# Four fused image layers on one core: the order and spacing of a wavelet layer's column products, and the start of the last pair's layers

## The chip, the cores and the metric

The kernel runs on one core of a Trainium2 chip. The core has five engines, each with its own instruction queue, worked off in order: TensorE (PE; its weight loads are listed apart as PEld), VectorE (DVE), ScalarE (ACT), GpSimd (POOL) and SyncE (SP), which here only issues DMAs. Engines wait for one another through semaphores. Data lies in SBUF (128 partitions) and in PSUM, where TensorE writes its sums; sixteen DMA engines move data between DRAM and SBUF.

The metric is the device time of one execution in microseconds. Comparisons use medians of several runs.

## What is computed

Four layers, each on a group-normalized input and added back to it. The input is 8 images of 64 channels, 128 x 128, in float32.

```python
# layer 0: adder convolution, 3x3
out[o] = relu(b[o] - abs(patches - w[o]).sum(-1))
# layer 1: spline activation for each channel
out = scale_base * silu(x) + scale_sp * einsum('bhwck,ck->bhwc', bspline_basis(x), coef) + bias
# layer 2: wavelet convolution
ll, ch, cv, cd = haar_dwt(x)                     # 4 subbands of 64 x 64
t = stack of the 4 subbands, transposed          # 256 channels
t = conv2d(t, dw_w, dw_b, groups=256, pad=1)     # depthwise 3x3
t = conv2d(t, pw_w, pw_b, pad=0)                 # 256 -> 256, 1x1
t = conv2d(t, cv_w, cv_b, pad=1)                 # 256 -> 256, 3x3
out = haar_idwt(gelu(t), transposed back)
# layer 3: nearest of 512 embeddings for each pixel
out = embed_weight[argmin(squared_dist(x_pixel, embed_weight))]

x = x + layer0(gn(x)); x = x + layer1(gn(x)); x = x + layer2(gn(x)); x = x + layer3(gn(x))
```

## The kernel before

Two images lie on the 128 partitions (2 x 64 channels): a pair. Four pairs are worked off.

**Layer 0 and its planner.** The adder layer takes by far the most time. ScalarE makes |x - w| for one channel and tap as a tile of 128 x 4096 (L821), VectorE makes maxima max(x, w) (L774) or a maximum fused with an addition (L844); TensorE sums the 64 channels of each tile with a selecting matrix into PSUM (L809). `layer0` holds a planner: clocks for PE, ACT and DVE, advanced by assumed costs (`COSTS` and constants), pick which engine gets the next tile and write the instruction order of the three engines out by hand. Some nine tiles (`buf`, `wide`, x) are in flight. A pass (16 output channels of a chunk of 32 rows) has 144 taps (`TAPS`).

**Layers beside it.** While layer 0 of pair n runs, layers 1 to 3 of pair n-1 run beside it in generators that are advanced in *steps*: `STEPS` gives the steps of layer 1, layer 2, the statistics of a raw pair and layer 3. The steps are spread evenly over the 16 passes of a pair (L755 to L757), so that one step comes about every two taps. Each generator notes its events under step numbers (`at(step, f, ...)`), and `spread_out` issues them in the order of the steps on all engines.

**Layer 2 beside.** `layer2_beside` works on 8 chunks of 16 image rows, `EACH` = 56 steps apart (b is a chunk's first step). For a chunk: `load` brings input rows (xin, one buffer), `columns` and `rows` make the subbands on VectorE, `depthwise` their 3 x 3 sums on VectorE. The 1 x 1 and 3 x 3 convolutions are one, by a fast scheme along the columns (an even and an odd output column from four products): `columns_of` makes the input v of product kind m (one buffer), `products` multiplies it on TensorE with weights u, which `load_u2` brings from DRAM for each of the 16 product events of a chunk (384 KB, one buffer, so a load waits until the product before it is done). A kind's four events gather in one PSUM tile `mm` (one buffer); the `take_` functions move it into g: `take_first` to `take_fourth` for kinds 0 to 3. Then come `gelu` on ScalarE, `inverse` (wavelet back) on TensorE, `add` to xa on VectorE, statistics, and `store`, a DMA to x_dram; xa (one buffer) is loaded by `load_x`. All these loads and stores are issued by SP, in the order that a scheduler gives them, and so are layer 0's stores of y (L673) and of channel sums (L621) and loads of st (L631).

**Last pair.** After layer 0 has ended, `layer1`, `layer2` and `layer3` work on the last pair alone, with all of its x in SBUF. `layer1` takes 16 units (half chunks); TensorE forms its sums in pa and pb (L953). `layer2` starts with `haar` of the first chunk and the first four rows of the second, put between the steps of the group norm; then `begin` (ACT) and `depthwise` (DVE) for each subband (KS = 1, 2, 3, 0), `products` for one half of the output bands (`oab`), and so on; its PSUM holds three tiles of two banks (`l2_ps`) and two of one bank (`l2_pi`). `take` moves a half into g, `two_inverses` and `two_adds` finish the chunk before. `layer3` prepares four rows first (`prepare`, `squares`, `take_squares`), then goes row by row: TensorE distances (L1227), ScalarE and VectorE the smallest (L1233, L1237, L1241), GpSimd fetches the embedding (L1242).

## Time and profile before

| what | us |
|---|---|
| three runs | 18358.89, 18349.82, 18328.94 (median 18349.82) |
| the profiled execution | 18391.41 |
| its span, first to last instruction | 18389.7 |
| first pair's layer 0 alone | about 0 to 3640 |
| layers 0 and beside it layers 1 to 3 of three pairs | about 3640 to 17274 |
| of that, layer 2 beside | about 4547 to 6480, 9150 to 11110, 13800 to 15740 |
| last pair alone: layer 1 | 17274 to 17535 |
| last pair alone: layer 2 | 17535 to 17977 |
| last pair alone: layer 3 | 17977 to 18390 |

The mean granted TensorE clock was 0.985 of full speed. A row of the groups by line gives line, engine, operation, the tiles written and read, shape and count; then busy time and the mean of one in ns; then the idle time of the engine just before these instructions and who ended it. "SPq" marks the issue of a DMA by SP, not its transfer. In a timeline a row has the start, the length, the instruction, and in brackets the idle time before it.

### The profile page before, as it was taken

What the parts mean: (1) busy time and instruction counts of PE and PEld (TensorE: products, weight loads), DVE (VectorE), ACT (ScalarE), POOL (GpSimd) and SP (SyncE); (2) the same over time, 40 slices, a digit from 0 to 9 for tenths busy, and PEclk for the clock granted to TensorE, in tenths of its full rate; (3) what the DMA queues carried; (4) which work ended last, traced back from release to release, by engine and by line L of the source; (5) the groups of instructions that cost most, each with busy time, mean ns of one, the idle gap of its engine ahead of it and who ended that gap; (6) DMA issues with size and microseconds to landing.
All of it is one profiled execution on the core that took longest, in us unless ns stands there. A gap on an engine that the chain in (4) does not pass through costs nothing.

```text
span 18389.7 us, 338059 instructions
## 1 busy us (share of the span) xinstructions
PE 17822.3 (97%) x150418; PEld 6142.1 (33%) x150418; DVE 17676.9 (96%) x13410; ACT 17162.3 (93%) x6556; POOL 3386.7 (18%) x1866
## 2 busy tenths in 40 slices
PE   8999999999999999999999999999999999999998
PEld 2222222222333323332233333233223333222364
DVE  8999999999999999999999999999999999999887
ACT  7999999999999999999999999999999999999924
POOL 1222222200000024430000002443000000344205
PEclk9999999999999999999999999999999999999997
DMA  7767777611111111011111111101111111110231
GB/s 146 132 124 137 132 130 137 130 40 40 43 48 49 44 39 26 23 31 38 41 41 48 53 43 39 29 23 29 42 39 44 45 53 43 28 28 21 66 107 42
DMA packets 454213, 1099.90 MB, mean 60 GB/s; under 512 B 72416, under 2 KB 234848, under 8 KB 395360
## 3 DMA queue, kind: packets, MB, share of 16 engines
q0 software_dynamic: 111792, 491.89, 15.2%
q1 hardware_dynamic: 340960, 586.39, 11.2%
q8 instruction: 1178, 19.30, 0.4%
q14 instruction: 283, 2.32, 0.0%
HBM read 526.58 MB, written 125.74 MB: 35 GB/s over the span
## 4 chain that ended last, share of the span: by engine, by line
PE 54%; DVE 26%; issue 11%; ACT 6%; DMA 2%; POOL 1%; SPq 0%; DVEq 0%; another core or an unknown queue 0%; ACTq 0%; POOLq 0%
PE ps L809 41%; DVE buf L774 13%; ACT buf L821 4%; PE mm L1511 4%; DVE buf L844 4%; PE pd L1666 2%; DVE r L1353 1%; DVE wide L774 1%; PE ps L1227 1%; PE m L1079 1%; DMA u<-u_dram 1%; DVE dw L1484 1%; DVE nd L1678 1%; DVE x L774 1%; PE pa L953 0%
## 5 line engine op out<-in xcount | busy, mean ns | idle before, releaser
L809 PE MATMUL ps<-buf,sel 128*32 128x512 f32 x112848 | 12574.1, 595 | 168.4 <-ACT buf L821 87.6
L821 ACT ACTIVATE buf<-wide,w 128x4096 f32<-128x4096 f32 x1901 | 6922.4, 3711 | 80.1 <-PE ps L809 79.3
L821 ACT ACTIVATE buf<-x,w 128x4096 f32<-128x4096 f32 x1823 | 6647.1, 3711 | 129.3 <-PE ps L809 123.6
L809 PEld LDWEIGHTS ps<-buf,sel 128*32 128x32 f32 x112848 | 3540.5, 110 | 8634.0 <-issue 7801.0
L774 DVE TENSOR_SCALAR buf<-x,w 128x4096 f32<-128x4096 f32 x1801 | 4166.2, 2357 | 75.2 <-PE ps L809 68.8
L774 DVE TENSOR_SCALAR buf<-wide,w 128x4096 f32<-128x4096 f32 x1731 | 4028.8, 2367 | 95.3 <-PE ps L809 89.7
L1681 POOL DMA_INDIRECT g<-in_L_conv_embed_weight,ix x768 | 1860.2, 2422 | 2390.0 <-issue 1170.8
L844 DVE SCALAR_TENSOR_TENSOR buf<-x,w,buf 128x4096 f32<-128x4096 f32 x440 | 1973.3, 4485 | 15.7
L658 POOL DMA_DIRECT2D y<-in_x x496 | 704.9, 2173 | 6961.4 <-ACT y L645 5343.3
L844 DVE SCALAR_TENSOR_TENSOR buf<-wide,w,buf 128x4096 f32<-128x4096 f32 x430 | 1928.4, 4485 | 15.3
L1511 PE MATMUL mm<-v,u 64*128 64x256 f32 x9216 | 1182.0, 401 | 142.1 <-DMA u<-u_dram 129.1
L1511 PEld LDWEIGHTS mm<-v,u 64*128 64x128 f32 x9216 | 893.4, 195 | 557.4 <-issue 239.3
L832 POOL DMA_DIRECT2D buf<-buf x203 | 508.0, 2503 | 2739.6 <-DVE buf L774 2363.2
L821 ACT ACTIVATE x<-wide,w 128x4096 f32<-128x4096 f32 x263 | 975.9, 3711 | 5.8 <-PE ps L809 5.8
L821 ACT ACTIVATE wide<-x,w 128x4096 f32<-128x4096 f32 x259 | 961.1, 3711 | 4.8 <-PE ps L809 4.8
L809 PE MATMUL ps<-wide,sel 128*32 128x512 f32 x7696 | 923.1, 594 | 11.4 <-ACT wide L821 4.6
L809 PE MATMUL ps<-x,sel 128*32 128x512 f32 x7776 | 927.2, 593 | 3.3 <-ACT x L821 1.9
L1484 DVE SCALAR_TENSOR_TENSOR dw<-sub,dws,dw 128x512 f32<-128x512 f32 (+2 forms) x768 | 573.4, 747 | 10.4
L1668 ACT ACTIVATE t<-emb,xsq 128x512 f32<-128x512 f32 x768 | 512.2, 718 | 42.3 <-DVE xsq L1659 23.8
L1678 DVE CUSTOM_DVE_ANT_0 nd<-pd,t 128x512 f32<-128x512 f32 x768 | 519.6, 677 | 32.5 <-ACT t L1668 17.0
L774 DVE TENSOR_SCALAR x<-wide,w 128x4096 f32<-128x4096 f32 x223 | 529.5, 2374 | 8.9 <-PE ps L809 8.8
L1680 DVE FIND_INDEX8 ix<-best,nd 128x8 uint32<-128x512 f32 x768 | 526.2, 685 | 0.0
(288 smaller groups left out, 10465.5 us busy)
## 6 DMA issues: line engine op xcount, KB each, us to landing
buf<-buf POOLq DMA_DIRECT2D x203, 2048.0 KB
u<-u_dram SPq DMA_DIRECT2D x512, 384.0 KB
z<-x_dram SPq DMA_DIRECT2D x192, 256.0 KB
x<-x_dram SPq DMA_DIRECT2D x96, 512.0 KB
raw<-in_x SPq DMA_DIRECT2D x32, 1024.0 KB
x_dram<-y SPq DMA_DIRECT2D x512, 64.0 KB
y<-in_x POOLq DMA_DIRECT2D x496, 64.0 KB
x_dram<-x SPq DMA_DIRECT2D x48, 512.0 KB
```

The source lines that it names most:

```text
L658: nc.gpsimd.dma_start(out=ys[p][at], in_=d, accum_op=ALU.add)
L774: nc.vector.tensor_scalar(ab, tap(p // OG, t), w[:, t : t + 1], None, ALU.max)
L809: nc.tensor.matmul(to, sel[:, M - 1 - m : 3 * M - 1 - m], rhs, start=(done % TAPS == 0), stop=((done + span) % TAPS == 0))
L821: nc.scalar.activation(ab, tap(p // OG, t), AF.Abs, bias=w[:, t : t + 1], scale=-1.0)
L832: nc.gpsimd.dma_start(out=into, in_=of, accum_op=ALU.add, max_dma_last_dim=8192)
L844: nc.vector.scalar_tensor_tensor(ab, tap(p // OG, t), w[:, t : t + 1], ab, ALU.max, ALU.add)
L1484: nc.vector.scalar_tensor_tensor(out, v, wt, out, ALU.mult, ALU.add)
L1511: nc.tensor.matmul(ps[:, i], u2[r, k % 2, di, :], vs[c, m][r, k, di : di + G, :], start=(k == 0 and di == 0), stop=(k == 3 and di == 2))
L1668: nc.scalar.activation(t, emb[:, 1], AF.Identity, bias=xsqs[j][:, n : n + 1])
L1678: nc.vector.tensor_tensor_reduce(nd, ps, t, 1.0, -FAR, ALU.subtract, ALU.max, mx[:, 0:1])
L1680: nc.vector.max_index(ix, mx, nd)
L1681: nc.gpsimd.indirect_dma_start(out=g[:, img, :], out_offset=None, in_=self.embed, in_offset=bass.IndirectOffsetOnAxis(ap=ix[:, 0:1], axis=0),)
```

## The change

Beside layer 0, a chunk's products are put three steps apart instead of two, a kind every 14 steps instead of 11, and the steps behind them (gelu, inverse, add, store) 12 later; layer 2 gets 514 steps. Kind 1, which goes into both columns, comes first: `take_first` makes both copies of it on ScalarE, `take_second` adds kind 0 to the even column.

In the last pair, the first wavelet rows are issued ahead of layer 1's last unit, in a pool of their own, and a small Silu activation ahead of layer 1; unit 0 of layer 1 has two ramps on VectorE instead of ScalarE. In layer 2 the first chunk is multiplied band by band for both halves, the second band by band for its first half; all PSUM tiles are of one kind (four of two banks). The last chunk's statistics are taken in two parts. Layer 3 prepares two rows first, then two, then four.

```diff
-STEPS = (208, 500, 24, 396)
+STEPS = (208, 514, 24, 396)
...
     "layer2_beside.products": {"PE": 2.95},
-    "layer2_beside.take_first": {"ACT": 1.0},
-    "layer2_beside.take_second": {"DVE": 1.18, "ACT": 1.0},
+    "layer2_beside.take_first": {"ACT": 2.0},
+    "layer2_beside.take_second": {"DVE": 1.18},
     "layer2_beside.take_third": {"DVE": 2.36},
     "layer2_beside.take_fourth": {"DVE": 1.18},
...
+                if n == 2 * NCH - 1:
+                    for part in first_rows:
+                        next(part)
...
-                        on_act = p < 1 + i
+                        on_act = p < (1 + i if n else 1 - i)
...
+    def haar(self, n, lo, hi, row, pool):
+        nc, S = self.nc, HW2
+        sub, inner = self.sub, slice(1, S + 1)
+        xv = self.x[n][:, lo:hi]
+        s, d = (pool.tile([P, R, S], F32, name=name, bufs=2)[:, 0 : hi - lo] for name in ("hs", "hd"))
+        nc.vector.tensor_tensor(s, xv[:, :, 0:W:2], xv[:, :, 1:W:2], ALU.add)
+        nc.vector.tensor_tensor(d, xv[:, :, 0:W:2], xv[:, :, 1:W:2], ALU.subtract)
+        out = [sub[:, k, row : row + (hi - lo) // 2, inner] for k in range(4)]
+        nc.vector.tensor_tensor(out[1], s[:, 0 : hi - lo : 2], s[:, 1 : hi - lo : 2], ALU.subtract)
+        nc.vector.tensor_tensor(out[2], d[:, 0 : hi - lo : 2], d[:, 1 : hi - lo : 2], ALU.add)
+        nc.vector.tensor_tensor(out[3], d[:, 0 : hi - lo : 2], d[:, 1 : hi - lo : 2], ALU.subtract)
+        yield
+        nc.vector.scalar_tensor_tensor(out[0], s[:, 0 : hi - lo : 2], self.m4, s[:, 1 : hi - lo : 2], ALU.add, ALU.add)
+        yield
+
+    def first_rows(self, pool):
+        S, G = HW2, R // 2
+        self.sub = pool.tile([P, 4, G + 3, S + 2], F32, name="sub")
+        self.m4 = pool.tile([P, 1], F32, name="m4")
+        self.nc.gpsimd.memset(self.sub[:, :, :, 0 : S + 2 : S + 1], 0.0)
+        self.nc.gpsimd.memset(self.sub[:, :, 0, 1 : S + 1], 0.0)
+        self.first_parts = [self.haar(0, 0, R, 1, pool), self.haar(1, 0, 4, 1 + G, pool)]
...
-            first = [haar(0, 0, R, 1), haar(1, 0, 4, 1 + G)]
-            fill = [part for part in first for _ in range(6)]
             mr = self.mr_tile()
             with tc.tile_pool(name="gn_ps", bufs=1, space=PSUM) as pg:
                 for _ in self.group_norm_steps(stats_in, mr, pg):
-                    for _ in range(2):
-                        if fill:
-                            next(fill.pop(0))
-            for part in fill:
-                next(part)
+                    pass
...
-            pp = ctx.enter_context(tc.tile_pool(name="l2_ps", bufs=3, space=PSUM))
-            pi = ctx.enter_context(tc.tile_pool(name="l2_pi", bufs=2, space=PSUM))
+            nc.vector.tensor_scalar(self.m4, mr[:, 0:1], -4.0, None, ALU.mult)
+
+            pp = ctx.enter_context(tc.tile_pool(name="l2_ps", bufs=4, space=PSUM))
...
-            def convolve(j, oab):
+            def convolve(j, oab, by_band=False):
                 pairs = open_pairs()
-                for n in range(2):
-                    for k in KS:
-                        products(j, oab, pairs, n, k)
+                order = [(n, k) for k in KS for n in range(2)] if by_band else [(n, k) for n in range(2) for k in KS]
+                for n, k in order:
+                    products(j, oab, pairs, n, k)
                 return pairs
...
+            def open_inverses(at):
+                both = pp.tile([P, 2, 2, G, S // 2], F32, name="m").rearrange("p a b r c -> p a (b r c)")
+                return {pos: both[:, n].rearrange("p (r c) -> p r c", c=S) for n, pos in enumerate(at)}
+
             def two_inverses(j, gs, at):
-                pys = {}
+                pys = open_inverses(at)
                 for pos in at:
-                    pys[pos] = pi.tile([P, G, S], F32, name="py")
                     for ab in range(2):
                         inverse(pys[pos], gs, pos, ab)
...
             begin(0, KS[:3])
-            pairs = open_pairs()
+            halves = [open_pairs() for _ in range(2)]
             for n, k in enumerate(KS):
                 if n == 3:
                     for part in first:
                         next(part, None)
                     begin(0, KS[3:])
                 depthwise(0, k)
-                for half in range(2):
-                    products(0, 0, pairs, half, k)
-            late = None
-            for j in range(NCH):
+                for oab, pairs in enumerate(halves):
+                    for half in range(2):
+                        products(0, oab, pairs, half, k)
+            transform(1)
+            begin(1, KS)
+            gs = []
+            for n, k in enumerate(KS):
+                depthwise(1, k)
+                if n in (1, 2):
+                    gs.append(take(halves[n - 1], n - 1))
+            late = (0, gs)
+            for j in range(1, NCH):
                 more = list(KS) if j + 1 < NCH else []
-                if j > 0:
-                    pairs = convolve(j, 0)
+                pairs = convolve(j, 0, j == 1)
                 if more:
                     transform(j + 1)
                     begin(j + 1, KS)
-                    for k in more[: 1 if j == 0 else 2]:
+                    for k in more[:2]:
                         depthwise(j + 1, k)
-                    del more[: 1 if j == 0 else 2]
-                if late:
-                    pys = two_inverses(*late, (0, 1))
+                pys = two_inverses(*late, (0, 1))
                 gs = [take(pairs, 0)]
-                if late:
-                    two_adds(j - 1, pys)
+                two_adds(j - 1, pys)
                 pairs = convolve(j, 1)
-                for k in more[:2]:
+                for k in more[2:]:
                     depthwise(j + 1, k)
-                del more[:2]
-                if late:
-                    pys = two_inverses(*late, (2, 3))
+                pys = two_inverses(*late, (2, 3))
                 gs.append(take(pairs, 1))
-                if late:
-                    two_adds(j - 1, pys)
-                for k in more:
-                    depthwise(j + 1, k)
-                if late:
-                    self.chunk_stats(stats, j - 1)
+                two_adds(j - 1, pys)
...
-            both = pp.tile([P, 2, 2, G, S // 2], F32, name="m").rearrange("p a b r c -> p a (b r c)")
-            pys = [pi.tile([P, G, S], F32, name="py") for _ in range(2)]
-            pys += [both[:, n].rearrange("p (r c) -> p r c", c=S) for n in range(2)]
+            pys = {**open_inverses((0, 1)), **open_inverses((2, 3))}
             for ab in range(2):
                 for pos in range(4):
                     inverse(pys[pos], gs, pos, ab)
+            by_parity = self.x[j].rearrange("p (r a) w -> p a r w", a=2)
             for pos in range(4):
                 add(j, pys[pos], pos)
-            self.chunk_stats(stats, j)
+                if pos % 2:
+                    for half in range(2):
+                        nc.vector.bn_stats(stats[:, 4 * j + pos - 1 + half, :], by_parity[:, pos // 2, half * G // 2 : (half + 1) * G // 2])
...
-            prepare(0, 0)
-            squares(0, 0, 4)
-            take_squares(0, 0, 4)
+            prepare(0, 0, 2)
+            squares(0, 0, 2)
+            take_squares(0, 0, 2)
+            prepare(0, 2, 2)
             prepare(0, 4)
             for n in range(NCH * R + LATE):
                 j, r = divmod(n, R)
-                if j == 0 and r in (1, 5, 9):
-                    squares(0, r + 3, r + 7)
-                    take_squares(0, r + 3, r + 7)
-                    if r < 9:
-                        prepare(0, r + 7)
+                if j == 0 and r in (1, 2, 5, 9):
+                    lo, hi = {1: (2, 4), 2: (4, 8)}.get(r, (r + 3, r + 7))
+                    squares(0, lo, hi)
+                    take_squares(0, lo, hi)
+                    if 1 < r < 9:
+                        prepare(0, hi)
...
             def take_first(c):
                 gs[c] = sp.tile([P, 2, 2, G, S], F32, name="g")
-                nc.scalar.copy(even_and_odd(c)[0], product_of(c, 0))
+                ps = product_of(c, 1)
+                for to in even_and_odd(c):
+                    nc.scalar.copy(to, ps)
 
             def take_second(c):
-                even, odd = even_and_odd(c)
-                ps = product_of(c, 1)
-                nc.vector.tensor_tensor(even, even, ps, ALU.add)
-                nc.scalar.copy(odd, ps)
+                even = even_and_odd(c)[0]
+                nc.vector.tensor_tensor(even, even, product_of(c, 0), ALU.add)
...
                     c = j - 1
-                    when = [(b + 11 * m + 3 + 2 * n, c, m, n // 2, n % 2) for m in range(4) for n in range(4)]
+                    kinds = ((1, take_first), (0, take_second), (2, take_third), (3, take_fourth))
+                    when = [(b + 14 * at_m + 3 + 3 * n, c, m, n // 2, n % 2) for at_m, (m, _) in enumerate(kinds) for n in range(4)]
                     for n, (step, *what) in enumerate(when):
                         at(when[n - 1][0] + 1 if n else b - 3, load_u2, *what)
                         at(step, products, *what)
-                    for m, take in enumerate((take_first, take_second, take_third, take_fourth)):
-                        at(b + 11 * m, columns_of, c, m)
-                        at(b + 11 * m + 11, take, c)
+                    for at_m, (m, take) in enumerate(kinds):
+                        at(b + 14 * at_m, columns_of, c, m)
+                        at(b + 14 * at_m + 15, take, c)
                     for oab in range(2):
-                        at(b + 46, gelu, c, oab)
+                        at(b + 58, gelu, c, oab)
                     for a in range(2):
-                        s = b + 48 + 9 * a
+                        s = b + 60 + 9 * a
                         at(s - (8 if a == 0 else 1), load_x, c, a, 0)
...
+            with tc.tile_pool(name="l2_first", bufs=1) as pool:
+                warm = self.small.tile([P, 1], F32, name="warm", tag="warm", bufs=1)
+                self.nc.scalar.activation(warm, self.bias1, AF.Silu)
+                later = self.stats_tile("later")
+                self.layer1(self.group_norm(stats.pop(last), by_tile=True), later, self.first_rows(pool))
+                self.early.close()
+                between = self.stats_tile("between")
+                self.layer2(later, between, pool)
             self.layer3(between, last)
```

Where lines are left out, the old inner function haar of layer2 and its memsets moved into the two new functions unchanged in what they compute, and calls pass the new pool.

## The prediction, made before the changed kernel was run

> **What bounds the kernel now.** I read the page first (engines, then the costliest groups), then the groups by line beyond it, then busy time by windows, then the instructions and waits of tile u, then the timeline of single waits.
>
> ```profile
> PE 17822.3 (97%) x150418; PEld 6142.1 (33%) x150418; DVE 17676.9 (96%) x13410; ACT 17162.3 (93%) x6556; POOL 3386.7 (18%) x1866
> ...
> L1511 PE MATMUL mm<-v,u 64*128 64x256 f32 x9216 | 1182.0, 401 | 142.1 <-DMA u<-u_dram 129.1 <-issue 5.8 <-ACT g L1537 4.1
> ```
>
> Three engines are nearly full, so only idle time that they share is worth anything. TensorE (PE) has 567 us of it, and one line, the products of layer 2, owns 142.1 us: TensorE stands waiting for the weights u to arrive from DRAM.
>
> ```profile
> 4547.00:6480.00 1933.00, 1872.38 (x16424) 731.92 (x16420) 1855.73 (x1149) 1835.95 (x543) 81.43 (x65) 0.98 0.17 46
> ...
> 6700.00:8200.00 1500.00, 1494.60 (x12749) 452.20 (x12753) 1481.26 (x1525) 1492.59 (x646) 689.51 (x305) 1.00 0.11 26
> ```
> ```profile
> 5213.00:5390.00 177.00, 177.00 (x1576) 69.60 (x1576) 174.92 (x108) 176.79 (x52) 0.00 (x0) 1.00 0.15 41
> ```
>
> Busy time by windows (length, then PE, PEld, DVE, ACT, POOL, clock, DMA). The first is layer 2 of the first pair beside the adder layer, the second layer 3 beside it: 97% of PE against 99.6%. The third lies inside layer 2 and has no wait for u: PE is full, ScalarE (ACT) and VectorE (DVE) almost. So the waits are the loss, and without them TensorE is the bound.
>
> ```profile
> 5186.45 0.33 SPq L1451 DMA_DIRECT2D xin<-x_dram  x1
> 5188.75 0.37 SPq L1574 DMA_DIRECT2D x_dram<-xa  x1
> 5191.10 0.37 SPq L1558 DMA_DIRECT2D xa<-x_dram  x1
> 5191.57 8.01 SPq L1500 DMA_DIRECT2D u<-u_dram  x2
> ```
> ```profile
> 5182.99 5.36 PE L809 MATMUL ps<-buf,sel 128*32 128x512 f32 x48
> 5194.92 4.29 PE L1511 MATMUL mm<-v,u 64*128 64x256 f32 x24 [6.56 <-DMA u<-u_dram]
> ```
>
> One wait, on SP's queue and on PE. The previous product had ended at 5183.0, so u's single buffer was free; but the load stood in SP's queue behind xin (waits for VectorE's rows), a store (waits for VectorE's additions at 5188.7) and xa (waits for that store to land, 2.3 us). It was issued at 5191.57 and landed 3.3 us later.
>
> ```profile
> L1511 PE MATMUL mm<-v,u x9216: 373/376/793, 4708.0 to 15641.2; 64*128 64x256 f32 x197
> ...
> PE mm L1511: 129.1, 42
> ```
> ```profile
> L1537 ACT COPY g<-mm 128x1024 f32<-128x1024 f32 x24 | 28.0, 1167 | 96.1 <-DVE g L1536 96.1
> ```
>
> 42 waits, 3.1 us each; a matmul's mean is 401 ns against a median of 376, because a product after a wait runs slow (4.29 us above, 2.86 without one). And ScalarE idles 96.1 us at L1537, held by VectorE's addition in the same step.
>
> **What a wait is worth.** Chunks of layer 2 are 56 steps; between first products at 4939.36 and 5159.83 lie 220.5 us, so a step is 3.94 us. Over the 21 chunk periods of the three pairs, a least-squares line gives 220.5 us plus 1.0 us for each us of wait: they cost their full length.
>
> **The change, part by part.**
>
> *Products three steps apart.* Between a product's end and the next one's start lay 2 x 3.94 - 2.86 = 5.0 us for a load that needs 0.4 to issue and 3.3 to land: 1.3 us to spare. Now it is 3 x 3.94 - 2.86 = 9.0, so 5.2 us to spare. Products, loads and bytes are the same in number (384 of each). I read where each load stands in SP's queue in both instruction orders, and what the transfers ahead of it wait for. Before, 34 loads stand behind VectorE work planned so late that, by 3.3 us landing and 2.3 us for a store, they cannot be in time; in the trace these make 73 us of wait, 2.15 each. After, 28 loads stand like that: 14 of a chunk's last products now fall among the next chunk's xin loads, 9 behind xa, 5 behind stores. At the same 2.15 us: 60 us. The 254 loads with only their own product ahead had 14 waits, 55 us, from the stores of y and the s_dram and st transfers; less 3.94 us each, 12 us stay. So waits for u go from 129 to 72: **-57 us**. Ends: none of the 28 waits (129 to 12, -117); all loss stays (0), if VectorE is later by a step.
>
> *Slow products.* 1182.0 x (1 - 376/401) = 74 us of L1511 is slow clock. In proportion to the waits: 74 x 57/129 = **-33 us** (0 to -67).
> The Trainium skill, "TensorE: Matmul & The Clock Gate", Part 1, says that an idle window of about 3.4 us halves the clock until a busy one has passed. The trace agrees in part: granted clock 0.98 in this stage against 1.00, and 4.29 us for 2.86, but a wait of 2.58 us at 4728.9 is followed by a slow product too. By its figure, an estimate is at most 3.4/2 = 1.7 us for each of 42 waits, 71 us, near the row's 74; the sum would not move.
>
> *Kind for both columns first.* Two ScalarE copies (L1531, L1537, 1.15 and 1.17 us) now stand together behind a product; VectorE's addition (1.22) is alone. Same instructions. The 96.1 us of ScalarE idle go; I take nothing for it on the path, because PE waits only 4.1 + 9.2 us for that copy; it keeps ScalarE from being the next bound. In exchange: the take of a kind now has two steps (7.9 us) to the next product that overwrites its only PSUM tile, instead of three; gelu stands one step behind the last take instead of two; the last inverse stands one step ahead of the copy that overwrites g, instead of nine. VectorE's takes started up to 9 us late against their step in the trace. Shifted by a step, those beyond the room (5.3 us before the third kind's 2.54 us of additions, 6.6 otherwise) make **+8 us** (0 to +30); ScalarE, if late at gelu, delays abs tiles that PE has buffered.
>
> *Planner.* 514 steps for 500 and moved costs give 3 more sum tiles (8020 tiles cost 14424 us of L809: 1.80 each), 2 fewer abs, 5 more maxima, 3 fewer fused: **+5 us** on PE, -7 on ACT, -2 on DVE.
>
> *Last pair, 1116 us behind the adder layer.* First rows: on VectorE hs to sub stood between the two norm products; PE's answer came at 17538.03 and was read at 17541.83, the second 0.5 late: **-4.3**. The 6.5 us go into layer 1, where VectorE was busy 154.7 of 180 us beside a full PE; without that cover they cost 6.5. First chunk by band for both halves: PE waited 3.0 twice for bands of 8.7 us VectorE time; four products a band (11.4 us) cover that, and when chunk 1's last band is ready (PE waited 5.2) 2 products are left instead of 5. That is 8.6 us if VectorE (185 of 200 us busy from 17700) keeps up: **-7** (0 to -11). Statistics by half: two of four beside PE, **-1.0**. Two rows instead of four in layer 3: four of eight matmuls (1.84 us) and half an activation pair, **-1.3** (0 to -1.6). Layer 1: the instruction order puts Silu with its table load (1.29 + 1.23 us) ahead of the first squares, one ramp is gone (1.14): **+1.5** (-1 to +3). The warm-up activation became ScalarE's second instruction of the whole program, with Gelu loads behind it, so the load in the last pair stays: 0 for that part. Sum -12.
>
> Sum: -57 - 33 + 8 + 5 - 12 = -89 us. The profiled execution took 18391.4 us (span 18389.7); less 89 is 18302. It lay 41.6 us over the median of three runs, 18349.8; I forecast on that: **18261 us**.
>
> **The rivals.**
>
> *The waits go almost wholly* (chance 0.18). The 28 loads land in time if VectorE is at its step when they come; the chunk's end has no row work of its own yet. -117 - 67 + 8 + 5 - 12 = -183: 18167. Against it: before, 25 of 34 such loads did wait.
>
> *The loss changes owner* (0.21). Waits for u fall, but VectorE, 174.9 of 177 us busy in the clear stretch, or ScalarE sets the pace, or loads now come late at the chunk border: half of -90 is lost: -45 + 13 - 12 = -44: 18306, up to 18350. For it: VectorE's own idle (77 us in the first window) is hardly larger than PE's (61).
>
> *Slower* (0.09): PSUM's single mm tile. If VectorE, no longer given time by PE's waits, runs more than 5.3 us behind its steps throughout, each of its three takes a chunk holds back the next product, and the tiles behind it on PE. At 3 us more than the room for 72 takes it is +216 us, with -57 - 33 + 5 - 12 of the sum +119: 18469. Against it: its lateness had a median near 2 us.
>
> **How the numbers follow.** The forecast (18215 to 18300) has 0.52. What can be told from no change is 0.2%, 37 us. Faster: 0.52 + 0.18 + under half of 0.21: 0.79. Same: 0.12. Slower: 0.09. The range takes in the two cases on its sides and leaves the slower one out: 18165 to 18350; the last pair's layer 3 runs at a clock near 0.8 that may move it by 15 us, half the spread of the runs.
>
> **What would show it.** Right: L1511's idle from u near 70 us or less, its mean near 390 ns, ScalarE's copies without 96 us of idle, chunk periods near 221 us; in the last pair, no PE wait of 3 us in the first chunk and the norm of layer 2 some 4 us shorter. Wrong: waits of L1511 on VectorE's or ScalarE's g of tens of us, u waits at the last product of chunks above 60 us, or `ps` waiting on buf from either engine more than its 168 us.

## The result, and the profile after

| | us |
|---|---|
| before, median of six runs | 18343.63 (18326.50 to 18358.89) |
| after, median of six runs | 18162.22 (18157.57 to 18188.25) |
| ratio after / before | 0.9905, 95% interval 0.9892 to 0.9918 |
| forecast | 18261 (range 18165 to 18350) |

The change is 181 us faster, twice the 89 us of the forecast's sum. The profiled execution after took 18174.1 us (span 18172.4), close to its median; that of before lay 48 us above its own, so the two profiles differ by 217 us. All lines below are of after unless the text names another kernel; its product line is L1516 (L1511 before), its load of u L1505, of xin L1456. First the engines and the costliest products on the page.

```profile
PE 17725.0 (98%) x150466; PEld 6115.0 (34%) x150466; DVE 17665.0 (97%) x13415; ACT 17155.7 (94%) x6554; POOL 3450.7 (19%) x1866
...
L809 PE MATMUL ps<-buf,sel 128*32 128x512 f32 x112944 | 12564.7, 594 | 142.6 <-ACT buf L821 57.8
...
L1516 PE MATMUL mm<-v,u 64*128 64x256 f32 x9216 | 1147.1, 393 | 76.2 <-DMA u<-u_dram 60.3
```

TensorE's busy time fell by 97 us. The products stand 76 us instead of 142, and are 35 us shorter; the sums of the adder layer stand 142.6 us instead of 168.4. The same two windows as before (columns: length, PE, PEld, DVE, ACT, POOL, clock, DMA share, GB/s):

```profile
4547.00:6480.00 1933.00, 1905.94 (x16908) 738.63 (x16904) 1912.78 (x1179) 1893.93 (x560) 73.08 (x65) 0.99 0.17 46
6700.00:8200.00 1500.00, 1482.70 (x12658) 447.11 (x12650) 1475.54 (x1516) 1484.73 (x638) 680.43 (x304) 1.00 0.10 27
```

In layer 2 beside the adder layer TensorE is busy 98.6% instead of 96.9%, and ScalarE and VectorE work 58 and 57 us longer in it. The instructions and waits of tile u, and ScalarE's copies by lines:

```profile
L1516 PE MATMUL mm<-v,u x9216: 373/376/792, 4706.1 to 15515.9; 64*128 64x256 f32 x197
...
PE mm L1516: 60.3, 28
```
```profile
L1538 ACT COPY g<-mm 128x1024 f32<-128x1024 f32 x48 | 52.9, 1169 | 24.7 <-PE py L1569 24.6
```

Of 42 waits for u (129.1 us), 28 are left (60.3 us). ScalarE's 96 us behind VectorE's addition are gone; its copies now wait 24.6 us for the inverse. One of the waits left, on SP's queue and on TensorE:

```profile
9659.25 0.32 SPq L1456 DMA_DIRECT2D xin<-x_dram  x1
9659.67 0.37 SPq L1505 DMA_DIRECT2D u<-u_dram  x1
```
```profile
9653.37 5.33 PE L809 MATMUL ps<-buf,sel 128*32 128x512 f32 x48
9662.93 4.55 PE L1516 MATMUL mm<-v,u 64*128 64x256 f32 x24 [4.23 <-DMA u<-u_dram]
```

It is a chunk's last product. The one before had ended at 9651.7, but the load of u stood behind xin, which VectorE released at 9659.2. As the forecast had read from the order, 14 of these loads stand directly behind xin; eleven of them came late, nine by more than 0.5 us (24.1 us together).

**Where the time went, by stages.** The end of the last sum came 154.6 us earlier (17274.5 to 17119.9), although the first pair's layer 0, which no edit touches, ended 14.6 us later in this profile (start of its last y, L645: 3636.5 for 3621.9). From there to the last sum the gain is 169.1 us. Then the last pair: layer 1 261.6 to 261.3, layer 2 441.2 to 434.5, layer 3 412.4 to 356.7. The last number is strange, since layer 3 was hardly touched; the first experiment settles it.

### The profile page after: what moved, and what is told of

The parts are those of the page before. It is cut to its first block, busy times and chain, and to the rows that moved or that the text cites. A ratio compares the mean times of both kernels' runs of the same rounds, so it can differ in the third digit from the quotient of the medians.

```text
span 18172.4 us, 338264 instructions
## 1 busy us (share of the span) xinstructions
PE 17725.0 (98%) x150466; PEld 6115.0 (34%) x150466; DVE 17665.0 (97%) x13415; ACT 17155.7 (94%) x6554; POOL 3450.7 (19%) x1866
## 4 chain that ended last, share of the span: by engine, by line
PE 51%; DVE 27%; issue 11%; ACT 8%; DMA 2%; POOL 0%; SPq 0%; DVEq 0%; ACTq 0%; POOLq 0%
PE ps L809 39%; DVE buf L774 13%; ACT buf L821 6%; DVE buf L844 4%; PE mm L1516 4%; PE pd L1672 1%; PE m L1080 1%; DVE dw L1489 1%; DVE wide L774 1%; DVE r L1358 1%; DMA buf<-buf 1%; PE ps L1230 1%; DVE x L844 1%; DVE x L774 1%; ACT t L1674 1%
## 5 line engine op out<-in xcount | busy, mean ns | idle before, releaser
L809 PE MATMUL ps<-buf,sel 128*32 128x512 f32 x112944 | 12564.7, 594 | 142.6 <-ACT buf L821 57.8
L809 PEld LDWEIGHTS ps<-buf,sel 128*32 128x32 f32 x112944 | 3547.9, 110 | 8589.2 <-issue 7829.1
L844 DVE SCALAR_TENSOR_TENSOR buf<-x,w,buf 128x4096 f32<-128x4096 f32 x417 | 1870.2, 4485 | 14.8
L844 DVE SCALAR_TENSOR_TENSOR buf<-wide,w,buf 128x4096 f32<-128x4096 f32 x409 | 1834.2, 4485 | 14.5
L1516 PE MATMUL mm<-v,u 64*128 64x256 f32 x9216 | 1147.1, 393 | 76.2 <-DMA u<-u_dram 60.3
L832 POOL DMA_DIRECT2D buf<-buf x203 | 546.5, 2694 | 2713.2 <-DVE buf L774 2321.0
L1516 PEld LDWEIGHTS mm<-v,u 64*128 64x128 f32 x9216 | 871.9, 190 | 485.2 <-issue 299.4
L809 PE MATMUL ps<-x,sel 128*32 128x512 f32 x7760 | 928.3, 594 | 4.8 <-DVE x L844 4.4
L809 PE MATMUL ps<-wide,sel 128*32 128x512 f32 x7664 | 917.2, 593 | 8.5 <-ACT wide L821 5.5
L1674 ACT ACTIVATE t<-emb,xsq 128x512 f32<-128x512 f32 x768 | 516.6, 727 | 39.1 <-DVE best L1684 28.7
L774 DVE TENSOR_SCALAR wide<-x,w 128x4096 f32<-128x4096 f32 x219 | 516.8, 2360 | 6.6 <-PE ps L809 6.6
```

What stands on the lines that cost most here:

```text
L774: nc.vector.tensor_scalar(ab, tap(p // OG, t), w[:, t : t + 1], None, ALU.max)
L809: nc.tensor.matmul(to, sel[:, M - 1 - m : 3 * M - 1 - m], rhs, start=(done % TAPS == 0), stop=((done + span) % TAPS == 0))
L832: nc.gpsimd.dma_start(out=into, in_=of, accum_op=ALU.add, max_dma_last_dim=8192)
L844: nc.vector.scalar_tensor_tensor(ab, tap(p // OG, t), w[:, t : t + 1], ab, ALU.max, ALU.add)
L1516: nc.tensor.matmul(ps[:, i], u2[r, k % 2, di, :], vs[c, m][r, k, di : di + G, :], start=(k == 0 and di == 0), stop=(k == 3 and di == 2))
L1674: nc.scalar.activation(t, emb[:, 1], AF.Identity, bias=xsqs[j][:, n : n + 1])
```

## The experiments

Each kernel was timed beside runs of before on the same chip. Before's own median differed between the groups of runs (18326 to 18408), so differences are given as (ratio - 1) x 18344 us; after is -174 by this measure. An interval of a ratio is 16 to 28 us to either side, of a difference of two ratios up to 40. The last column is a second measure: the change, against before's profile, of the stage from the first pair's last y to the last sum in the one profiled execution; it leaves out the last pair and the first pair's layer 0. "Old" is before's layout of layer 2 beside, "new" after's; "no u" is a kernel that loads one tile of u once (experiment 4).

| kernel | ratio, 95% interval | us | stage in the profile, us |
|---|---|---|---|
| beside | 0.9908, 0.9892 to 0.9923 | -169 | -172 |
| lastpair | 0.9997, 0.9988 to 1.0006 | -6 | +2 |
| spacing | 0.9916, 0.9902 to 0.9929 | -154 | -160 |
| kinds | 0.9985, 0.9976 to 0.9994 | -28 | -28 |
| old, 507 steps | 0.9963, 0.9949 to 0.9976 | -68 | -68 |
| old, 514 steps | 0.9983, 0.9974 to 0.9992 | -31 | -34 |
| old, 521 steps | 0.9998, 0.9989 to 1.0007 | -4 | -14 |
| old, 528 steps | 0.9987, 0.9978 to 0.9996 | -24 | -27 |
| new, 521 steps | 0.9940, 0.9926 to 0.9953 | -110 | -112 |
| new, 528 steps | 0.9951, 0.9938 to 0.9965 | -90 | -79 |
| new, 535 steps | 0.9973, 0.9962 to 0.9983 | -50 | -54 |
| no u, old, 500 steps | 0.9934, 0.9920 to 0.9947 | -121 | -125 |
| no u, old with new kinds, 500 | 0.9935, 0.9922 to 0.9949 | -119 | -112 |
| no u, old, 514 | 0.9919, 0.9906 to 0.9933 | -149 | -145 |
| no u, new, 514 | 0.9889, 0.9874 to 0.9904 | -204 | -205 |
| no u, new, 528 | 0.9925, 0.9912 to 0.9939 | -138 | -132 |
| u by GpSimd, new, 514 | 0.9884, 0.9869 to 0.9899 | -213 | -199 |
| u by GpSimd, new, 528 | 0.9926, 0.9912 to 0.9939 | -136 | -137 |

**1. Which half of the change: beside, lastpair.** The first takes from the diff only the part beside layer 0, the second only the rest. Main lines of the first:

```diff
-STEPS = (208, 500, 24, 396)
+STEPS = (208, 514, 24, 396)
...
+ps = product_of(c, 1)            # take_first, and take_second
+for to in even_and_odd(c):
+    nc.scalar.copy(to, ps)
...
+when = [(b + 14 * at_m + 3 + 3 * n, c, m, n // 2, n % 2) for ...]
```

> The part beside layer 0 alone (three steps apart, kind 1 first, 514 steps); the last pair as before. The change as a whole took 181 us off the median, and 56 of the 217 us between the two profiled executions lie in layer 3 of the last pair, which the change hardly touches. Theory A: that layer 3 difference is a clock that varies from run to run, and the gain lies beside layer 0. Then this kernel is 165 to 175 us faster than before, u waits near 60 us, and the last pair's layer 3 takes some 360 to 412 us, whichever clock it meets. Rival B: the last pair's edits bring layer 3's 56 us. Then this one gains only about 115 to 125 us and its layer 3 takes 412 us again.

> The last pair's edits alone; beside layer 0 everything as before, u waits near 129 us. Theory A: 8 to 15 us faster than before (layer 2 some 7 us shorter, as between the two profiles; layer 3 by 1 to 2 us apart from the clock). Rival B: 55 to 70 us faster, layer 3 near 357 us again.

-169 and -6: theory A. Layer 3 of the last pair, in its old form, took 361.2 us in beside, 360.9 in spacing and 358.0 in kinds; in its new form 360.2 in lastpair. So the 56 us between the two profiles were not the change's: before's one profiled execution had met a lower clock there (last section).

**2. Spacing or order of kinds: spacing, kinds.**

```diff
 # spacing: three apart, old takes, 514 steps
-when = [(b + 11 * m + 3 + 2 * n, ...
+kinds = ((0, take_first), (1, take_second), (2, take_third), (3, take_fourth))
+when = [(b + 14 * at_m + 3 + 3 * n, ...
 # kinds: two apart, new takes, 500 steps
+kinds = ((1, take_first), (0, take_second), (2, take_third), (3, take_fourth))
+when = [(b + 11 * at_m + 3 + 2 * n, ...
```

> Three steps apart alone, with the old order of the kinds and their old takes; last pair as before. Theory A (the spacing gives the loads room and is all that counts beside layer 0): within 15 us of the kernel with the whole beside part, u waits near 60 us, while ScalarE's idle before its copy into the odd column stays near 96 us and costs nothing. Rival C (the order of kinds relieves ScalarE and VectorE, and so the adder tiles that TensorE waits for): 40 us or more slower than the whole beside part, with idle at the adder layer's sums near the 168 us of before rather than the 143 of after.

> Kind 1 first alone, products two steps apart as before, 500 steps; last pair as before. Theory A: u waits stay near 129 us and the time within 20 us of before. Rival C: 40 us or more faster, with ScalarE's 96 us of idle gone and less idle at the adder layer's sums.

Groups by line, spacing first, then kinds (the product line of each, and ScalarE's copy in spacing):

```profile
L1511 PE MATMUL mm<-v,u 64*128 64x256 f32 x9216 | 1151.3, 394 | 82.9 <-DMA u<-u_dram 72.4 <-issue 7.4 <-ACT g L1537 2.4
```
```profile
L1537 ACT COPY g<-mm 128x1024 f32<-128x1024 f32 x24 | 28.0, 1166 | 68.6 <-DVE g L1536 63.6 <-PE ps L809 5.1
```
```profile
L1511 PE MATMUL mm<-v,u 64*128 64x256 f32 x9216 | 1172.8, 399 | 132.9 <-DMA u<-u_dram 118.9 <-issue 12.5 <-DVE v L1496 1.2
```

Spacing alone gives 154 of the 169 us, though ScalarE still stands 68.6 us. Kinds alone gives 28, a little over theory A's 20, with the u waits hardly changed. But spacing's row shows 59 us less standing (idle time before them) than before's and 31 us shorter products, 90 in all. The sums stand 31 us less too (137.3 for 168.4), so some 33 us of its gain have no place yet. It also has 14 steps more.

**3. The number of steps alone: old layout with 507, 514, 521 and 528.** The added steps stay empty.

```diff
-STEPS = (208, 500, 24, 396)
+STEPS = (208, 507, 24, 396)      # 514, 521, 528
```

> Before with 514 steps for layer 2 instead of 500, all else as before (14 steps of the layer stay empty). Between the profiles of the spacing alone and of a kernel with the old spacing, waits for u fall by 54 to 57 us and products by 31 us of slow clock; the median fell by 155. Some 65 us are open. Theory F: the pacing of 514 steps (all other layers' steps a little closer together) brings them: 40 to 70 us faster than before, u waits still near 129 us. Theories D and E: within 15 us of before.

> Before with 507 steps for layer 2 (7 of them empty). 514 steps alone gave 16 to 47 us. Theory F (closer steps gain, in proportion): 10 to 20 us faster than before. Theory J (the number of steps only shifts which loads of u meet other transfers in SP's queue, a draw of some 30 us either way): anything from 35 us faster to 35 us slower, with u waits that follow.

> Before with 528 steps for layer 2 (28 empty). Theory F: 45 to 80 us faster than before, twice what 514 steps gave. Theory J: within 35 us of before, u waits between 95 and 160 us.

> Before with 521 steps for layer 2 (21 empty). Old layout so far, against before: 507 steps 68 us faster, 514 31, 528 24. Theory J (a draw): between 0 and 70 us faster, u waits 100 to 130 us. It is the fourth draw of the old layout, for the mean.

-68, -31, -4, -24: no proportion, so theory F falls as it was put, as do D's and E's 15 us at 514 and theory J's 35 us at most at 507. But a change of the step count alone moves the time by up to 68 us. The products' row with 514 steps:

```profile
L1511 PE MATMUL mm<-v,u 64*128 64x256 f32 x9216 | 1173.5, 399 | 124.8 <-DMA u<-u_dram 99.3 <-DVE v L1496 11.0 <-ACT g L1537 7.5
```

So 30 of the 69 us by which after's u waits are shorter than before's come with the 14 steps already. The time does not follow these waits, though: they are 114.6 us at 507 steps, 99.3 at 514, 121.0 at 521 and 120.5 at 528.

**4. What the waits for u are worth: one tile of u for all products.**

```diff
-t = u2s[c, m, oab, half] = sp.tile([P, 2, 3, P], F32, name="u2")
-nc.sync.dma_start(out=t, in_=...)
+if not u2s:
+    u2s[0] = sp.tile([P, 2, 3, P], F32, name="u2")
+    nc.sync.dma_start(out=u2s[0], in_=...)
...
-u2 = u2s.pop((c, m, oab, half))
+u2 = u2s[0]
```

> Before, but layer 2 beside loads one u tile once and all its products use that one, so its output is not layer 2's: it leaves out 381 loads of u of a pair's 384 in three pairs, and thus every wait for them. Theory D (a wait leaves a trail: ScalarE and VectorE stand too, and TensorE finds fewer tiles ready afterwards): the gain is much more than 129 us of waits and 74 us of slow products, 260 to 290 us, and the kernel ends within 25 us of the same edit at three steps apart; idle at the adder layer's sums falls by 40 us or more. Theory E (two steps apart the products themselves crowd out the adder tiles): 200 us gained, 50 us or more slower than the same edit at three steps apart, idle at the sums stays near 170 us.

> After, with the same edit: one u tile loaded once for all products of layer 2 beside (output not layer 2's). It shows what the 60 us of u waits that are left cost. Theory D: 60 us of waits, 37 us of slow products and a trail: 120 to 140 us faster than after, near 18030. Theory E: 100 us faster at most, and 50 us or more ahead of the same edit at two steps apart.

> Before with kind 1 first (two steps apart, 500 steps) and with one u tile loaded once for all products of layer 2 beside (output not layer 2's). Without waits for u, two steps apart with the old order of kinds lost 0.45% (some 83 us) against three apart with the new order; in its profile ScalarE still stood 108.8 us at the copy behind VectorE's addition, and the sums stood 187 us instead of 120. Theory H (ScalarE's stand at that copy is on the path once u is not): the new order alone takes 40 to 80 us off the kernel without u loads at the old order, and the sums' idle falls by 30 us or more. Theory E (the spacing itself): less than 20 us.

> Before with 514 steps, and one u tile loaded once for all products of layer 2 beside (output not layer 2's). With 500 steps this edit gained 121 us against before, at the new layout with 514 steps 203. If the open 75 us are the step count's: 185 to 215 us faster than before. If they are the spacing's: 110 to 140 us faster, and products waiting for VectorE's v by 35 us or more, as with 500 steps.

> After with 528 steps and one u tile loaded once (output not layer 2's). With 514 steps: 203 us faster than before. Theory J through SP's queue alone: 185 us or more. If 528 steps cost the sums beside layers 1 and 3 whatever u does, as GpSimd's loads suggest (212 at 514, 135 at 528): 120 to 150 us faster.

Theory D falls: at 500 steps a kernel that never waits for u gains 121 us, not 260, and less than the 203 us of waits and slow products that before's rows held. Theory E's 200 us fall with it, though its difference came: the new layout is 55 us ahead at equal steps (204 for 149, the last pair's 6 included). The old layout's -149 with 514 steps lies between the two cases set for it. Groups by line, sums and products: the old layout without u (514 steps), the same with the new kinds (500 steps), then the new layout without u.

```profile
L809 PE MATMUL ps<-buf,sel 128*32 128x512 f32 x112752 | 12554.5, 594 | 184.6 <-ACT buf L821 115.3 <-DVE buf L774 39.1 <-DMA buf<-buf 14.9
L1512 PE MATMUL mm<-v,u 64*128 64x256 f32 x9216 | 1135.6, 390 | 34.4 <-DVE v L1496 34.4
```
```profile
L809 PE MATMUL ps<-buf,sel 128*32 128x512 f32 x112848 | 12570.9, 595 | 178.8 <-ACT buf L821 71.9 <-DVE buf L774 55.2 <-DMA buf<-buf 27.1
L1512 PE MATMUL mm<-v,u 64*128 64x256 f32 x9216 | 1140.6, 391 | 52.4 <-DVE v L1496 51.1 <-ACT buf L821 1.1 <-ACT g L1534 0.2
```
```profile
L809 PE MATMUL ps<-buf,sel 128*32 128x512 f32 x112944 | 12560.2, 594 | 120.3 <-ACT buf L821 56.0 <-DVE buf L774 46.4 <-DVE buf L844 6.4
L1517 PE MATMUL mm<-v,u 64*128 64x256 f32 x9216 | 1134.7, 390 | 47.1 <-DVE g L1549 17.4 <-DVE g L1543 17.1 <-DVE g L1553 9.0
```

Two things are to be seen. Once u is never late, the products wait for others in its place: for VectorE's v in the old layout (34.4), for VectorE's takes in the new one (43.5), which in after hardly showed. And the sums stand 184.6 us in the old layout against 120.3 in the new one. Of these 64 us, 45 lie between the first and last products of the three pairs' layer 2, 10 beside layer 3, and 11 in the first pair's layer 0, which no edit touches. Inside layer 2 of the third pair, sums alone, without u: old (514 steps), new, and old with new kinds (500 steps); then spacing, with u:

```profile
L809 PE MATMUL ps<-buf,sel 128*32 128x512 f32 x10005 | 1122.2, 595 | 20.2 <-ACT buf L821 20.2
```
```profile
L809 PE MATMUL ps<-buf,sel 128*32 128x512 f32 x10340 | 1152.1, 593 | 1.0 <-ACT buf L821 1.0
```
```profile
L809 PE MATMUL ps<-buf,sel 128*32 128x512 f32 x10128 | 1131.9, 594 | 9.2 <-DVE buf L774 8.3 <-DVE buf L844 0.8
```
```profile
L809 PE MATMUL ps<-buf,sel 128*32 128x512 f32 x10340 | 1153.2, 594 | 4.7 <-ACT buf L821 4.7
```

So it is the order of kinds, far more than the spacing, that ends the sums' waits for ScalarE's tiles in layer 2. Summed over the three pairs:

| sums wait for ScalarE in layer 2, us | old kinds | new kinds |
|---|---|---|
| two apart, 500 steps, no u | 32.9 | 0.9 |
| two apart, 500 steps, with u | 19.9 (before) | 0.3 (kinds) |
| two apart, 514 steps, with u | 28.7 | not run |
| 514 steps, no u | 46.8 (two apart) | 1.0 (three apart) |
| three apart, 514 steps, with u | 16.3 (spacing) | 0.2 (after) |

Two steps apart, however, VectorE is late in ScalarE's place: without u the sums stand 26.7 us in layer 2 for other tiles than ScalarE's, nearly all VectorE's, and v is later (51.1 us for 34.7 with the old kinds). The kernel stays at -119, and theory H falls. Only with both the new order and three steps are both waits small. No run has three steps with the old kinds and without u, so how the gain of the pair divides there is open.

**5. Is the gain bound to 514 steps: new layout with 521, 528 and 535.**

> After with 521 steps instead of 514. New layout so far, against before: 514 steps 174 to 181 us faster, 528 90. Theory J (514 was a lucky draw; the layout itself is worth about the 90 us forecast): 80 to 140 us faster than before. Theory E (the spacing itself is worth 150, 528 is an exception): 150 to 190 us faster.

> After with 528 steps instead of 514. Theory F: 20 to 40 us faster than after, so some 205 us faster than before. Theory J: within 25 us of after (155 to 205 us faster than before): with three steps' room few loads are near enough to a limit for the draw to matter.

> After with 535 steps instead of 514. Theory J: 60 to 140 us faster than before. Theory E: 150 to 190 us faster. Theory K (more than 72 steps in a pass of 144 taps put some steps at neighbouring taps, so products come closer again): with 72.7 steps a pass no better than 528, 90 us or less, u waits above 90 us.

-174 at 514, then -110, -90, -50: 514 is the best of the four, as theory J said, though with a trend and not as a draw: J's range holds at 521, and not at 528 (155 to 205) or 535 (60 to 140). Theory E's 150 to 190 came at neither 521 nor 535. K's time came at 535, its u waits above 90 us did not (82.2); 521 shows that the loss begins under 72 steps a pass, so K's limit isn't its start. Layer 3 beside the adder layer, third pair, sums in after (514) and in after with 535 steps:

```profile
L809 PE MATMUL ps<-buf,sel 128*32 128x512 f32 x9764 | 1094.4, 594 | 5.8 <-ACT buf L821 3.8 <-DVE buf L774 1.8
```
```profile
L809 PE MATMUL ps<-buf,sel 128*32 128x512 f32 x9588 | 1078.1, 595 | 17.7 <-ACT buf L821 13.6 <-DVE buf L844 4.1
```

With more steps, layers 1 and 3 are pressed into less time, and there the sums stand longer: summed over the three pairs, 18.7 us beside layer 3 at 514 and 54.0 at 535, 39.5 and 65.7 beside layer 1. And u waits rise again, to 94.9 us at 528. At equal counts new minus old is -143 (514), -106 (521) and -66 (528), the last pair's 6 included.

**6. u by another queue: u_pool, u_pool528.** Both are the new layout.

```diff
-nc.sync.dma_start(out=t, in_=self.u2_dram[...])
+nc.gpsimd.dma_start(out=t, in_=self.u2_dram[...])
```

> After, with the loads of u issued by GpSimd instead of SP, so that they no longer stand behind xin, xa and stores. Theory A (the order in SP's queue makes the waits that are left): waits at a chunk's last product (24 us in after) and third product (14 us) go, u waits fall under 30 us and the time by 40 to 80 us. Rival G: GpSimd's own queue (merges of buf that wait for VectorE, slower issue) brings as many waits or more: no gain, or up to 100 us slower.

> After with the loads of u issued by GpSimd and 528 steps instead of 514. With 514 steps GpSimd's loads were 212 us faster than before. If 528 steps lose through SP's queue (u waits rose from 60 to 95 us in after): within 30 us of 212, 180 to 215 us faster than before. If they lose elsewhere (layers 1 and 3 beside layer 0, the sums): 130 to 150 us faster.

-213 at 514 steps, the fastest whole kernel here: 39 us ahead of after by the ratios. The intervals of the two overlap, so that it beats after is likely and not shown. Its products' row:

```profile
L1516 PE MATMUL mm<-v,u 64*128 64x256 f32 x9216 | 1135.8, 390 | 45.3 <-issue 38.6 <-PE ps L809 5.5 <-DVE v L1501 0.9
```

45 us of standing are left, and to 38.6 of them the profile gives no cause ("issue"). All 45 stand at the first product of a kind, where VectorE's takes held the products without u; where they are longer than 1.1 us, the load of u had been issued 13 to 19 us before, so u is not what was late. With 528 steps it loses 77 us, and the new layout without u loses 66: the larger part of what 528 steps cost doesn't go through SP's queue or u.

## Why the prediction was half the gain

The runs split after's -174 us thus, at 514 steps. The uncertainty is some 17 us in the first and the last row and 40 to 50 in the two between, which join three or four ratios. The profiles' stages give a second split; its last row is layers 1 and 2 of the last pair.

| part | measured | by the profiles | forecast |
|---|---|---|---|
| 14 steps more, nothing else | -31 | -34 | +5 |
| waits for u and slow products: no-u gain old (149 - 31 = 118) less new (204 - 174 = 30) | -88 | -75 | -57 - 33 = -90 |
| new layout where u never waits: -204 + 149, less the last pair's 6 | -49 | -60 | +8 |
| last pair | -6 | -7 | -12 |

Two terms failed, the planner's and that of the kinds. The waits for u, which the forecast was about, came out near their price. Its signs of being right all came: 60.3 us from u, products of 393 ns on average, ScalarE's copies without the 96 us, chunk periods of 219.6 us on average. But none of them looked at the number of steps.

*Products three steps apart: right*, in its mechanism and near its size. 129.1 us of waits became 60.3 (forecast 72), mostly at places read from SP's queue: eleven waits at a chunk's last product, six at its third. But 30 us of the fall came with the 14 steps, which the forecast had not foreseen. *Slow products: right*: the row fell by 34.9 us. But without any wait for u it fell by no more than 41.9 (1182.0 to 1140.1, old layout with 500 steps), so the end of -67 was out of reach. The 71 us that the prediction estimated for all these waits from the Trainium skill's page "TensorE: Matmul & The Clock Gate", Part 1, were too much in the same way, as a gain: in that kernel 34.7 us of waits for v stood in u's place.

*What a wait is worth: misread.* From the trace, the line through the 21 chunk periods (between chunks' first products) comes out as 220.3 us plus 1.3 us, not 1.0, for each us that the products stood. The slow products lie within these periods, so the sum counted them a second time when it took -33 on top: by this line -57 of waits would be about -75 with the slow products in it.

*Planner (+5): wrong.* The step counted tiles and priced them, and put nothing on when the beside work comes. The number of steps alone was worth -31 at 514 (0.9983, 0.9974 to 0.9992). In its profile the waits for u fell to 99.3 us; why that count falls well is open.

*Kind for both columns first (+8): wrong, in what it took for nothing.* The price of the takes was small: what products stand for others than u rose from 13.0 to 15.9 us. But ScalarE's idle was put at nothing because PE hardly waited for its copy. PE also waits for ScalarE's tiles at the sums, and there the order of kinds took 19.9 us in layer 2 to 0.3 by itself, and the kernel gained 28 us. Without u the order alone gains nothing (-119 for -121), since VectorE is late in its place; with three steps the pair gains the table's 49 to 60. The profile of before had the sign of it: L809 stood 87.6 us for ScalarE, more than for anyone else, and these 87.6 were 57.8 afterwards.

```profile
L809 PE MATMUL ps<-buf,sel 128*32 128x512 f32 x112848 | 12574.1, 595 | 168.4 <-ACT buf L821 87.6 <-DVE buf L774 53.6 <-DMA buf<-buf 16.1
```

*Last pair (-12).* Norm of layer 2: right. The read of TensorE's answer no longer stands behind hs to sub, and the first product comes 13.2 us after the norm's start instead of 17.5: -4.3. First chunk by band (-7): wrong. TensorE and VectorE in the timeline of after:

```profile
17394.44 1.23 PE L1080 MATMUL m<-v,u 64*128 64x256 f32 x4 [9.67 <-DVE v L1064]
...
17445.73 1.23 PE L1080 MATMUL m<-v,u 64*128 64x256 f32 x4 [6.04 <-issue]
...
17487.70 3.78 PE L1080 MATMUL m<-v,u 64*128 64x256 f32 x16 [4.45 <-issue]
```
```profile
17435.84 6.26 DVE L1059 SCALAR_TENSOR_TENSOR dw<-sub,dws,dw 128x512 f32<-128x512 f32 x8
...
17444.94 0.69 DVE L1108 TENSOR_TENSOR g<-m,ma 128x512 f32<-128x512 f32 x1
```

The waits of 2.99, 3.00 and 5.22 us are gone, and 6.04 and 4.45 have come: 0.7 us gained. Both halves of the first chunk hold all four PSUM tiles, so the second chunk's first product starts when `take` has read one of them (L1108 ends at 17445.63), and `take` stands behind two bands of `depthwise`. That this is the cause is read from the order and the times, not tried. The rest is small: layer 1 -0.3 for +1.5; in layer 3 nothing beyond the spread of 356.6 to 361.2 of runs at the same clock.

*The rivals.* "The waits go almost wholly" had the time, 18167, by luck: 60 us of waits stayed, and the rest of the gain came elsewhere. "The loss changes owner" is true of the kernels without u, where v and the takes take over 34 and 44 us. "Slower", takes that hold back products, did not come about: they hold products 43.5 us only where u never waits.

*Open.* Why 514 steps suit the new layout better than 521 or 528 is shown only in part as to where it is lost (sums beside layers 1 and 3, waits for u), and not why. In the old layout the four counts stay unexplained. The new layout was not run with 500 or 507 steps. Two tiles of u, loaded earlier, were not tried.

## What to carry to other kernels

The idle time at a wait is no price: here, with three engines at 93 to 97%, the next wait stood behind it. A kernel with the transfer left out gives the price at once (121 us here for 203 in the rows). Where work is paced by a count of steps, that count is a change of its own; try a layout at several counts before crediting it. And look first at the stages that a change doesn't touch: what differs there belongs to the run. Here the first pair's layer 0 ended anywhere from 3605 to 3645 us in the 20 profiles.

## What had not been expected of the hardware

The last pair's layer 3 has two speeds that go with the group of runs, not with the kernel. Each group of the experiments ran on another chip, so it may be the chip or the time; the runs don't tell. Windows over it in the old layout with 521 and with 514 steps, whose layer 3 is the same code:

```profile
17960.00:18309.00 349.00, 323.12 (x1080) 161.31 (x1078) 328.10 (x1034) 221.06 (x348) 241.98 (x256) 0.83 0.17 49
```
```profile
17930.00:18349.00 419.00, 362.20 (x1090) 179.38 (x1090) 332.47 (x1037) 223.09 (x352) 242.94 (x257) 0.75 0.14 41
```

The same instructions, 349 and 419 us, at a granted clock of 0.83 and 0.75. In the groups of runs whose before had a median of 18326 or 18332, layer 3 took 357 to 361 us in each of eight kernels; in those with 18392 or 18408, 417 to 426 in each of ten. The profiles of before (412 us) and after (357) fell on either side. The forecast had given this clock 15 us; between the two speeds lie some 60 us, a third of the gain under study. Why the clock differs is open.
